# Preparing a chunk's two layouts with VectorE's 32x32 transposes instead of TensorE's, norms spread through DRAM

## The chip, the core and the metric

One core of a Trainium2 chip runs the whole program in one launch. The metric is the time of one execution on the device, in microseconds (us). Engines are named as the profile names them: PE (TensorE, matrix multiplication; PEld is its weight load), DVE (VectorE), ACT (ScalarE), POOL (GpSimd) and SP (SyncE, which here only issues transfers). Each engine works through its own instructions in order; semaphores make it wait for others.

## The reference

The input `x` has four images of 32 channels, 128x128 pixels, float32. Layer 0 is an attention among the positions that share a channel block: the image is regrouped so that 2x2 pixels become four channels, rows of a matrix `q` with 128 rows and 4096 columns per image, and the rest is

```python
xs = x.reshape(B, C, h, R, w, R).transpose(0, 1, 3, 5, 2, 4).reshape(B, C * R * R, h, w)
q = xs.reshape(B, C * R * R, hw)                   # 4 x 128 x 4096
energy = jnp.einsum('bci,bcj->bij', q, q)          # 4096 x 4096 per image
d = jnp.sqrt(jnp.diagonal(energy, axis1=1, axis2=2))
attn = jax.nn.softmax(energy / (d[:, :, None] * d[:, None, :]), axis=-1)
out = gamma * jnp.einsum('bcj,bij->bci', q, attn) + xs   # then back to the image
```

So every one of the 4096 columns of `q` is divided by its own norm before the product, and the values use `q` as it is. Layer 1 takes the image's pixels as 8 x 8192 tokens of 128 features: a linear attention over 8 heads after a layer norm, added to the tokens, then a layer norm and a mixture of 8 experts with the best two of a softmax router, added again. Only layer 0's preparation of `q` is touched by the change.

## The kernel before, in words

The kernel goes through the four images (batches, b = 0 to 3). A batch has 4096 columns in 8 chunks of 512 (`CH`); two chunks are prepared together, so a batch has four preparations, kc = 0 to 3. In this text a prepared pair is called "a chunk" where its preparation is meant. `prep` (lines 282 to 350) makes two layouts of it. `qT` holds columns on the partitions (128 columns by 128 channels, four such blocks per 512 columns) and is used as values; `qn` holds channels on the partitions with 512 normalised columns and is used on both sides of the energy product.

`prep` loads image rows into `xx` with four transfers of 128 KB (`load_tokens`, line 274), transposes them on PE into PSUM (`ptq`, line 313) and copies them with DVE into `qT` (line 302). DVE squares `qT` and sums the squares (lines 324, 325), POOL raises the sums to the power -1/2 (`pow_neg_half`, line 163), DVE scales `qT` with the result into `qs` (line 338), PE transposes `qs` (`ptn`, line 346), and ACT copies that into `qn` (line 344). Between these steps stand `yield`s.

`attend` (line 417) is the main work. For each chunk i and each jc up to i it multiplies `qn` with `qn` (`pe`, line 556), ACT takes the exponential into `pr` and sums its rows (line 559), and PE multiplies `pr` with `qT` (`po`, line 440). The energy is symmetric, so only half of it is made; for the other half DVE transposes `pr` in 32x32 blocks into `F` (line 369), SP writes `F` to DRAM as `blocks` (line 483) and reads it back regrouped as `G` (line 491), and `transposed_share` (line 371) multiplies `G` with `qT` into `pg` and adds that to the accumulator `o` of chunk jc (line 385), while ACT sums `G` (line 380). `po` becomes `o` by a copy of ACT (line 445).

The order of the instructions on PE, DVE, ACT and SP is that in which the program issues them (`manual_schedule`, line 1329). A step of `attend` is one exponential; `after(n, f)` issues `f` n steps later, and a share of `G` is issued when `clock`, which counts 128-column pieces of PE's work, has gone `LAG` = 57 pieces on. Other work runs along as generators: a list `timed` holds (generator, begin, end, count), with begin and end in per cent of a batch's `clock`, and `count` turns are spread over that window. `attend` yields twice in a step; the list `moved` of the generators to advance is made at the first of the two and used at both:

```python
for half, _ in enumerate(chain(attend(b, states[b]), ...)):
    if half % 2 == 0:
        moved = []
        ...                       # generators whose turn it is
    for steps in moved:
        next(steps, None)
```

So one turn takes a generator past two `yield`s. Layer 1 of the batch before runs in the same way (`layer1`, line 602): `close_rows` divides `o` by the softmax's sums and adds it to the tokens `T` (`divide`, line 703), then follow statistics on DVE, a power on POOL, a normalisation on ACT, PE products, the sorting of tokens by expert through DRAM (POOL's indirect transfers), the experts' products `pys`, and the sum with the tokens that ACT fetches back from DRAM (`fetch`, line 1097).

Buffers that the steps speak of: PSUM has two banks for `pe`, one for `po`, two for `pg` and three for everything else (`pt`, handed out by `hold`, line 191); `pr` has six buffers, `qT` five, `qn` ten, `xx` one; `T` holds a batch's rows, which `input_rows` (line 593) loads.

## Time and profile before

| what | us |
|---|---|
| three runs | 1710.81, 1708.52, 1704.93 |
| median | 1708.52 |
| the profiled execution | 1712.1 |
| its span, first to last instruction | 1710.3 |
| PE busy in it | 1651.3 |
| DVE busy | 934.7 |
| ACT busy | 925.2 |
| POOL busy | 512.0 |

The mean granted clock of TensorE is 0.994. A line of the groups reads: line of the kernel, engine, operation, names out<-in, size, xcount | busy us, mean ns of one | idle time of the engine just before them, and what ended it. A line in the order of time reads: start, length, engine, line, operation, [idle before it <- what ended that]. Ends of matmuls are modelled, and a matmul is shown until its last result, so two that follow each other overlap in the rows; the time that one takes of PE is read from start to start. "SPq" is a transfer's issue on SP's queue.

### The profile page before, as it was taken

The numbers are of one execution on the slowest core, as the hardware profiler recorded it, in microseconds if no ns is written. First come the engines' busy times: TensorE is split into PE (matmuls) and PEld (weight loads), VectorE is DVE, ScalarE is ACT, GpSimd is POOL, SyncE is SP. The second block draws the span as 40 slices with busy tenths as digits, with TensorE's granted clock in tenths as the row PEclk, the third lists the DMA queues.
The fourth block names the chain that finished last, engine by engine and source line by source line (L and its number), as shares of the span: only waits on it lengthen the run. The fifth ranks groups of instructions, "written<-read, shape, count | busy, mean of one in ns | idle before, by whom it ended". The sixth has DMA issues, their size and how long they took to land. (4 is left out here: it accounts for less than half of the span.)

```text
span 1710.3 us, 21189 instructions
## 1 busy us (share of the span) xinstructions
PE 1651.3 (97%) x5458; PEld 875.0 (51%) x5458; DVE 934.7 (55%) x2443; ACT 925.2 (54%) x2893; POOL 512.0 (30%) x553
## 2 busy tenths in 40 slices
PE   8999999999999999989999999999999999998897
PEld 5444444455554555445554455544555455554543
DVE  4433344467485345478478334547748533455686
ACT  3555445566565555546575555545556555554476
POOL 1000000011027425460015632544102642445166
PEclk9999999999999999999999999999999999999999
DMA  4665768876569888985568888997646987996001
GB/s 141 190 210 172 201 209 243 259 217 186 162 194 282 252 257 250 281 261 178 160 191 244 262 264 247 261 263 220 186 150 191 286 260 236 257 277 151 7 11 40
DMA packets 240681, 355.25 MB, mean 208 GB/s; under 512 B 27312, under 2 KB 155312, under 8 KB 226480
## 3 DMA queue, kind: packets, MB, share of 16 engines
q1 hardware_dynamic: 220048, 314.91, 62.4%
q0 software_dynamic: 12288, 25.19, 5.1%
q10 hardware_dynamic: 8224, 13.77, 2.8%
q8 instruction: 46, 0.75, 0.2%
q14 instruction: 75, 0.61, 0.1%
HBM read 183.64 MB, written 173.15 MB: 209 GB/s over the span
## 5 line engine op out<-in xcount | busy, mean ns | idle before, releaser
L559 ACT ACTIVATE pr<-pe 128x512 f32<-128x512 f32 (+1 forms) x576 | 322.4, 560 | 548.8 <-PE pe L556 432.0
L440 PE MATMUL po<-pr,qT 128*128 128x512 f32 (+3 forms) x1152 | 551.3, 560 | 3.9 <-ACT o L445 3.2
L556 PE MATMUL pe<-qn,qn 128*128 128x512 f32 x896 | 461.5, 597 | 3.8 <-ACT pr L559 2.7
L375 PE MATMUL pg<-G,qT 128*128 128x512 f32 x880 | 450.9, 594 | 4.1 <-DMA G<-blocks 4.1
L369 DVE STREAM_TRANSPOSE F<-pr 128x512 f32<-128x512 f32 x440 | 306.0, 702 | 163.3 <-ACT pr L559 140.9
L440 PEld LDWEIGHTS po<-pr,qT 128*128 128x128 f32 x1152 | 215.9, 191 | 250.4 <-issue 223.0
L380 ACT ACTIVATE junk<-G 128x512 bf16<-128x512 f32 x440 | 273.0, 621 | 2.6 <-DMA G<-blocks 2.6
L375 PEld LDWEIGHTS pg<-G,qT 128*128 128x128 f32 x880 | 167.2, 191 | 200.6 <-issue 185.1
L1122 POOL DMA_INDIRECT yb<-ys,place x192 | 185.9, 968 | 254.5 <-ACT pr L559 82.1
L995 POOL DMA_INDIRECT xs<-xn,place x192 | 186.3, 970 | 158.9 <-ACT pr L559 81.4
L556 PEld LDWEIGHTS pe<-qn,qn 128*128 128x128 f32 x896 | 153.9, 191 | 112.9 <-issue 100.0
L385 DVE TENSOR_TENSOR o<-o,pg 128x512 f32<-128x512 f32 x110 | 75.4, 685 | 192.3 <-PE pg L375 155.3
L164 POOL TENSOR_TENSOR rn<-ss,neg_half 128x8 f32<-128x8 f32 (+1 forms) x17 | 26.9, 1586 | 334.1 <-DVE ss L325 334.0
L559 ACT ACTIVATION_READ_ACCUMULATOR pr<-pe 128x1 f32 x576 | 112.2, 195 | 0.0
L1031 ACT ACTIVATE xn<-pys 128x256 f32<-128x256 f32 x120 | 45.3, 377 | 113.0 <-PE pys L1064 71.4
L164 POOL TENSOR_TENSOR rsf<-dm_f,neg_half 128x8 f32<-128x8 f32 (+1 forms) x15 | 26.2, 1748 | 233.6 <-DVE sv_f L636 233.6
L1057 PEld LDWEIGHTS pys<-ew_sb,xn 128*128 128x128 f32 x468 | 69.4, 191 | 49.0 <-issue 42.6
L556 PE MATMUL pe<-qn 128*128 128x512 f32 (+3 forms) x256 | 90.5, 436 | 4.0 <-ACT pr L559 3.3
L380 ACT ACTIVATION_READ_ACCUMULATOR junk<-G 128x1 f32 x440 | 84.5, 192 | 0.0
L164 POOL TENSOR_TENSOR rsa<-dm_a,neg_half 128x8 f32<-128x8 f32 x16 | 26.4, 1648 | 188.6 <-DVE sv_a L636 188.2
L1040 DVE COPY xn<-pys 128x256 f32<-128x256 f32 x60 | 25.4, 424 | 93.5 <-ACT xn L1031 72.3
L1040 DVE COPY result<-pys 128x256 f32<-128x256 f32 (+1 forms) x60 | 24.6, 410 | 90.4 <-ACT xn L1031 46.3
(212 smaller groups left out, 1653.5 us busy)
## 6 DMA issues: line engine op xcount, KB each, us to landing
blocks<-F SPq DMA_DIRECT2D x108, 1024.0 KB
G<-blocks SPq DMA_DIRECT2D x432, 256.0 KB
xn<-xs SPq DMA_DIRECT2D x114, 128.0 KB
below<-F SPq DMA_DIRECT2D x31, 384.0 KB
G<-below SPq DMA_DIRECT2D x124, 96.0 KB
out_dram<-acc SPq DMA_DIRECT2D x128, 64.0 KB
xx<-in_x_dram SPq DMA_DIRECT2D x62, 128.0 KB
ys<-xn SPq DMA_DIRECT2D x60, 128.0 KB
```

The source lines that it names most:

```text
L164: pinned(nc.gpsimd.tensor_tensor(dst, src, neg_half.to_broadcast(list(src.shape)), ALU.pow))
L369: f()
L375: nc.tensor.matmul(pg.rearrange("p (a f) -> p a f", a=4), st["qT"][i][:, ib, :], G[:, :, ib], start=(ib == 0), stop=(ib == NJ - 1),)
L380: nc.scalar.activation(junk, G[:, :, ib], AF.Copy, accum_out=st["sums"][:, NJ * i + ib, jc : jc + 1])
L385: nc.vector.tensor_tensor(o, o, pg.rearrange("p (a j c) -> p a j c", a=4, c=S), ALU.add)
L440: nc.tensor.matmul(row["po"][:, lo:hi], qT[blk // NJ][:, blk % NJ, :], w, start=start, stop=(row["left"] == 0))
L556: nc.tensor.matmul(pe[:, c0:], qn[jc][:, ts(j, P)], qn[i][:, c0:], start=True, stop=True)
L559: nc.scalar.activation(pr[:, c0:], pe[:, c0:], AF.Exp, accum_out=sums[:, t, i : i + 1]).ins
L995: inst = nc.gpsimd.indirect_dma_start(xs[h], offset(place[:, i, k : k + 1]), xn[:, k, :], None)
L1040: nc.vector.tensor_copy(result[:, :n], p[:, 2 * P : 2 * P + n * D].rearrange("p (j c) -> p j c", c=D))
L1057: nc.tensor.matmul(p[:, 2 * P + j * D : 2 * P + j * D + D], bufs[4 + g % 2][:, j, :], weights[:, bass.ds(begins[2 * (g % 2) + j], D)], sta ...
L1122: inst = nc.gpsimd.indirect_dma_start(yb[k // 4][:, i, k % 4, :], None, ys, offset(place[:, i, k : k + 1]))
```

## The change

Both layouts are now made without PE, except for the first chunk of the first batch.

- `load_quarters` loads image rows so that 32 partitions hold the 32 channels and four such groups hold four rows each (`xa`, four transfers of 128 KB, two pieces of 2 KB per partition in each). `turn_quarters` transposes them with DVE in 32x32 blocks straight into `qT`: four instructions of 256 elements per partition for a chunk. The columns come in another order than before.
- Squares, sums and the power stay. The power's result lies in a [128, 32] tile whose other columns hold ones; DVE transposes it, ACT's queue writes it to DRAM (`norms`, 16 KB) and reads it back twice, each time spread over 64 partitions (`wide`). DVE multiplies image rows with `wide` into `qn`: four instructions of 64 partitions by 512 (`scale`).
- The image rows for that are loaded as before, as `xx` from the second batch on, after the quarters have been turned, into the same buffer. In the first batch they go straight into `T`, and `input_rows` no longer loads `T` there.
- `ahead` is the number of `yield`s between a transfer and its use: five, and two for the second chunk.
- The first chunk has `prep_first`: DVE transposes the quarters, the scaled `qs` goes through PE and ACT as before. The spare transposes that keep PE running are 40, before 22.
- The accumulator `o` has its columns in the order of `pg`: ACT permutes when it copies `po` into `o`, the add of `pg` is plain, the adds of `back` and `divide` permute.
- The windows of the preparations and their counts change: 26 turns instead of 12 or 13.

```diff
+    def load_quarters(b, kc, queues=(nc.sync, nc.sync)):
+        xa = xin.tile([P, 2, 2, 2, HW2, 2], F32, tag="xx", name=f"xa_{b}_{kc}")
+        halves = x[b].rearrange("c (s g) w -> c s (g w)", s=2)
+        for a in (0, 2, 1, 3):
+            first_row = 16 * kc + 4 * a
+            queues[a // 2].dma_start(
+                xa[ts(a, S)].rearrange("p s k r w e -> p s (k r w e)"),
+                halves[:, :, first_row * W : (first_row + 4) * W],
+            )
+        return xa
+
+    def turn_quarters(s, xa, qT):
+        for k in range(2):
+            nc.vector.transpose(
+                qT[:, s, 2 * k : 2 * k + 2, :].rearrange("p h (e r c) -> p r (h e) c", e=2, r=2),
+                xa[:, s, k].rearrange("p r (h t) e -> p (r h) e t", h=2),
+            )
...
+    def squares(b, kc, s, qT, ss):
+        sq = work.tile([P, NJ, P], F32, tag="qs", name=f"sq_{b}_{kc}_{s}", bufs=2)
+        nc.vector.tensor_tensor(sq, qT[:, s], qT[:, s], ALU.mult)
+        nc.vector.tensor_reduce(ss[:, ts(s, NJ)], sq, AX.X, ALU.add)
...
     def prep(b, kc, st):
...
-                    nc.tensor.transpose(
-                        pt[:, ts(2 * jj + r2, P)], xx[:, k : k + 2, :, r2].rearrange("p k w -> p (k w)"), ident
-                    )
...
+        ahead = 2 if b == 0 and kc == 1 else 5
+        xa = load_quarters(b, kc)
+        if b == 0:
+            load_tokens(st["T"][:, ts(kc, 8), :], b, 8 * kc, 8)
+            xx = rows_of_image(b, kc, st)
+        for _ in range(ahead):
+            yield
+        qT = chunks_of(b, kc, st)
+        for s in range(2):
+            turn_quarters(s, xa, qT)
+            yield
+        if b > 0:
+            xx = xin.tile([P, 8, HW2, 2], F32, tag="xx", name=f"xx_{b}_{kc}")
+            load_tokens(xx.rearrange("p k w r -> p k (w r)"), b, 8 * kc, 8)
...
+        def scale(s, spread, view):
+            qn = channels(b, kc, s, st)
+            own = slice(s * 64, s * 64 + 64)
+            for r2 in range(2):
+                nc.vector.tensor_tensor(
+                    qn[ts(r2, 64)].rearrange("p (j a t) -> p a j t", a=4, t=S),
+                    xx[own].rearrange("p (a k) (h t) r -> p r a (k h) t", a=4, h=2)[:, r2],
+                    view(spread[own]),
+                    ALU.mult,
+                )
+        norm = norms[kc % 2]
+        for s in range(2):
+            squares(b, kc, s, qT, ss)
+            if s == 1:
+                pow_neg_half(norm[:, : 2 * NJ], ss)
+            yield
+        for _ in range(ahead - 2):
+            yield
+        turned = stat.tile([P, S], F32, tag="turned", name=f"turned_{b}_{kc}")
+        nc.vector.transpose(turned, norm)
         yield
+        kept = dram.tile([P, S], F32, tag="norms", name=f"norms_{b}_{kc}")
+        nc.scalar.dma_start(kept, turned)
+        for _ in range(ahead):
+            yield
+        wide = work.tile([P, CH], F32, tag="qs", name=f"wide_{b}_{kc}", bufs=2)
+        for s in range(2):
+            nc.scalar.dma_start(
+                wide[ts(s, 64)].rearrange("p (a f) -> p a f", a=4),
+                kept.rearrange("(a q) t -> a (q t)", q=S)[:, ts(s, P)].partition_broadcast(64),
+            )
+        for _ in range(ahead):
+            yield
+        for s in range(2):
+            scale(s, wide, lambda ap: ap.rearrange("p (a j t) -> p a j t", a=4, t=S))
+            yield
...
-                o = st["o"][jc].rearrange("p (j a c) -> p a j c", a=4, c=S)
-                nc.vector.tensor_tensor(o, o, pg.rearrange("p (a j c) -> p a j c", a=4, c=S), ALU.add)
+                nc.vector.tensor_tensor(st["o"][jc], st["o"][jc], pg, ALU.add)
...
-                    nc.scalar.activation(o, row["po"], AF.Copy)
+                    nc.scalar.activation(in_order(o), in_turn(row["po"]), AF.Copy)
...
-            for kc, begin, end in ((1, 0, 5), (2, 6, 20), (3, 25, 45)):
-                timed.append((prep(0, kc, states[0]), begin, end, 12))
+            for kc, begin, end in ((2, 6, 22), (3, 25, 48)):
+                timed.append((prep(0, kc, states[0]), begin, end, 26))
...
-            timed.append((prep(b + 1, 0, nxt), 65, 82, 13))
-            timed.append((prep(b + 1, 1, nxt), 87, 99, 13))
+            timed.append((prep(b + 1, 0, nxt), 52, 78, 26))
+            timed.append((prep(b + 1, 1, nxt), 80, 99, 26))
...
-            timed.append((prep(b + 1, 2, nxt), 2, 20, 13))
-            timed.append((prep(b + 1, 3, nxt), 30, 50, 13))
+            timed.append((prep(b + 1, 2, nxt), 1, 22, 26))
+            timed.append((prep(b + 1, 3, nxt), 28, 52, 26))
```

## The prediction

> **What bounds the kernel now.** I read the page's busy times and slices first, then the groups of instructions, then the order in time around the work that the change removes, and last the waits of that work.
>
> ```profile
> PE 1651.3 (97%) x5458; PEld 875.0 (51%) x5458; DVE 934.7 (55%) x2443; ACT 925.2 (54%) x2893; POOL 512.0 (30%) x553
> PE   8999999999999999989999999999999999998897
> DVE  4433344467485345478478334547748533455686
> DMA  4665768876569888985568888997646987996001
> ```
>
> PE is busy in 97% of the span and in nearly every slice; DVE and ACT are at 55% and 54%. So an instruction taken off PE is worth its own time, if nothing else makes PE wait. DMA is at nine tenths in several slices.
>
> The order in time around two of the removed groups, and the rows of the DVE work on both sides of the change:
>
> ```profile
> 1322.71 1.02 PE L375 MATMUL pg<-G,qT 128*128 128x512 f32 x2
> 1323.57 0.63 PE L313 MATMUL ptq<-ident,xx 128*128 128x128 f32 x4
> 1324.04 1.02 PE L556 MATMUL pe<-qn,qn 128*128 128x512 f32 x2
> ...
> 1354.62 1.02 PE L375 MATMUL pg<-G,qT 128*128 128x512 f32 x2
> 1355.48 0.60 PE L346 MATMUL ptn<-ident,qs 128*128 128x128 f32 x4
> 1355.91 1.02 PE L556 MATMUL pe<-qn,qn 128*128 128x512 f32 x2
> ```
> ```profile
> L369 DVE STREAM_TRANSPOSE F<-pr 128x512 f32<-128x512 f32 x440 | 306.0, 702 | 163.3 <-ACT pr L559 140.9 <-issue 14.8 <-DMA G<-blocks 5.5
> L513 DVE STREAM_TRANSPOSE F<-pr 128x128 f32<-128x128 f32 x186 | 44.0, 282 | 26.6 <-ACT pr L559 25.9 <-ACT junk L380 0.5 <-issue 0.2
> L709 DVE TENSOR_TENSOR df<-o,pbd 64x512 f32<-64x512 f32 x64 | 43.9, 686 | 8.6 <-PE pe L556 3.9 <-PE pbd L722 3.5
> L302 DVE COPY qT<-ptq 128x512 f32<-128x512 f32 x32 | 21.7, 679 | 33.1 <-PE ptq L313 26.7 <-PE pe L556 6.4
> L338 DVE TENSOR_TENSOR qs<-qT,rn 128x512 f32<-128x512 f32 x32 | 20.6, 682 | 1.5 <-POOL rn L164 1.5
> ```
>
> PE has no gap here. From start to start, four ptq transposes take 0.47 us of it and four ptn transposes 0.43 (the shown 0.63 and 0.60 overlap what follows). The places where PE did wait at this work, in the order of time:
>
> ```profile
> 726.98 0.72 PE L313 MATMUL ptq<-ident,xx 128*128 128x128 f32 x4 [1.38 <-DMA xx<-in_x_dram]
> 749.73 0.66 PE L346 MATMUL ptn<-ident,qs 128*128 128x128 f32 x4 [2.77 <-issue]
> 1135.20 1.10 PE L313 MATMUL ptq<-ident,xx 128*128 128x128 f32 x4 [3.77 <-issue]
> 1160.71 0.66 PE L346 MATMUL ptn<-ident,qs 128*128 128x128 f32 x4 [3.07 <-DVE o L385]
> ```
> ```profile
> 376.42 1.91 SPq L279 DMA_DIRECT2D xx<-in_x_dram  x4
> 1121.65 10.25 SPq L279 DMA_DIRECT2D xx<-in_x_dram  x4
> ```
> ```profile
> 490.00:500.00 10.00, 9.45 (x26) 4.47 (x25) 9.43 (x42) 4.83 (x15) 2.11 (x3) 1.00 0.76 211
> ```
>
> Two waits are for input rows that came late, two for DVE. The four loads of one chunk took 1.9 us to issue in a quiet stretch and 10.25 in a dense one, where SP waits for earlier transfers between them. The last row (columns: window, length, busy PE, PEld, DVE, ACT, POOL, clock, DMA share, GB/s) is the stretch where DVE is nearly full.
>
> **Removed from PE.** 16 chunks lose two ptq groups each and 15 lose two ptn groups (the first chunk keeps its own). Outside the start that is 30 x 0.47 = 14.1 us and 30 x 0.43 = 12.9 us, together 27.0, all on the path of an engine that is full. The four waits above, 1.38 + 2.77 + 3.77 + 3.07 = 11.0, lose the instructions that waited; I count them as gone here and price what is late next below. ACT loses 30 evictions of 0.59 (17.7 us), off the path. The permuted accumulator costs nothing: the permuted add at L385 takes 685 ns and the contiguous one at L524 684, so the change swaps equals; ACT's permuted copy into o is bounded by L445's 590 and L380's 621 ns, 32 x 0.03 = 1 us on an engine half idle.
>
> **The start.** PE's first pe starts at 13.62 us, after rows (5.70), transposes, copy, squares, sums, power, scaling. Without the first transposes and copies (5.70 to 8.38), but with four DVE transposes, three of which stand ahead of the first square, the first scaling ends about 1.4 us sooner: -1.4. The 40 spare transposes (0.2 us each by 22 in 4.4 us) fill 8 us in which PE has nothing; if they begin only at 5 us they end at 13 and the gain is gone. The second chunk uses two steps of distance, about 3 us for each of its two transfers, against 2.8 us from the last issue at 724.15 to use at 726.98: I take +1 (bounds 0 and 4, one late transfer of 3.6 us as at 1131.58 to 1135.20).
>
> **Added to DVE.** A 128x256 transpose lies between 282 ns (128x128) and 702 (128x512): 0.49, four a chunk, 1.97. Four scalings of 64x512 at 0.686 are 2.74, the norms' transpose at most 0.28, say 0.2. Against two copies and two scalings removed (2.72), a chunk costs DVE 2.2 us more: 33 us over 15 chunks. 55% becomes 57%; by itself hidden. It lies on a path in one place: for the chunk prepared in the window 28 to 52% of a batch, two of the transposes stand in DVE's order ahead of the statistics whose POOL result ACT awaits (ACT idle 4.15 us at 496.47, PE 0.55 at 498.74 already). 2 x 0.49 = 1 us each in batches 1 to 3: +3 (bounds 0 and 9, if the squares' 2.7 us also count).
>
> **The new waits.** The loop that advances a chunk's generator moves it twice per turn (the list of what moves is kept over the second half step), so five steps are 2.5 turns of 1/26 of the window. A batch is 405 us (ptq at 390.69, then 796.16), so transfer to use is 7.4 us in the window 80-99, 8.2 in 1-22, 9.3 in 28-52, 10.1 in 52-78; before it was 3.5 turns of 1/13: 13.1 us in 87-99. There the rows came 1.38 and 3.77 late, so they took 14.5 and 16.9 us from step to landing. With 7.4 us DVE, not PE, now stands 7.1 to 9.5 us at two chunks, before the transposes of pr, the adds of pg and the copies of pys that are queued behind. PE goes on while six pr tiles, two pg and three pt banks last; the pr tiles give some four steps of 2.58 us, 10 us, the pt banks less. Bounds 0 and 9.5; I take 3 each: +6. In these two chunks the first transpose also waits for a matmul two steps ahead (5.2 us), beside this wait, not on top. In window 1-22, the first issue stood 5.3 us behind its step before (3.5 turns of 1/13 of 2-20 are 19.6; 376.42 to 390.69 is 14.3), then 1.9 issue and 2.8 landing: 10.0 against 8.2, DVE waits 1.8; PE through the closing of layer rows 0 to 2, I take 1, three times: +3.
>
> ACT issues 45 DMAs (norms out, two rows back). An issue itself lies beside an ACTIVATE (313.41 within 313.19 to 313.79), cost nothing; a wait in it holds the exponentials queued behind, and PE after two pe banks. It waits for DVE's transpose, for the norms' landing, and for earlier SP transfers with the same semaphore. The 24 fetches of t2 by ACT show no PE wait; the largest unexplained ACT gap (4.53 us at 769.54) cost PE 3.05. Bounds 0 and 3.05 x 15 = 46; nearest are the 24 fetches, so a tenth: +4.
>
> SP issues 60 quarter loads more, 32 half-size loads of batch 0 less. Bytes: +8.4 MB quarters, +4.2 norms out and spread, -2.1 second read of batch 0: 10.5 of 355, 3%. SP's blocks and G transfers are queued behind these loads; PE waits 4.1 us for late G now (2.31 at 188.05). I take +2 (bounds -1 and 12 x 2.31 = 28).
>
> **Sum.** -27.0 - 1.4 - 11.0 = -39.4; +1 +3 +6 +3 +4 +2 = +19. The profiled execution took 1712.1 us (span 1710.3), so 1691.7; it lies 3.6 above the median of the runs, so 1688.
>
> Two rules of the Trainium skill speak against the change. "VectorE: DVE Perf Modes", section Rules for kernel authors, sends a 128x128 transpose to TensorE if PSUM will do; the row here is 0.47 us of a full PE plus 0.68 of DVE against about 0.98 of a DVE with room. If the rule held here, the 14.1 us would not be earned and the sum would be 1702. "DMA: Bandwidth & Descriptors", section Specifications, puts line rate at 512 B and more; the norms leave in rows of 128 B. No row of this trace shows that alone; were it to double the 2.8 us, ACT would wait half a microsecond for three chunks, and the sum would be 1690.
>
> **Rivals.** (1) All of the gain stays: DVE's waits end within PE's buffers, ACT's never bind. For it: in quiet stretches rows land in time, and DVE has 45% idle. Against: dense stretches. 1712.1 - 39.4 - 3.6 = 1669. (2) No difference: ACT's wait for norms or for SP's transfers costs PE 3.05 us at 12 chunks, 36.6: 1706. For it: order on ACT is strict, and two steps of 2.58 us is the shortest distance from norms out to norms back. Against: the fetches. (3) Slower: each of the 12 chunks of batches 1 to 3 holds DVE for its rows longer than PE's buffers last. It decides from 39.4 / 12 = 3.3 us of PE a chunk; at 4.53 it gives 1712.1 - 39.4 + 54.4 - 3.6 = 1723. For it: distances are halved, and DVE is full at 490. Against: outside 80-99 SP issued the rows in 2 to 3 us.
>
> **How the numbers follow.** Forecast 0.52 (1676 to 1702), rival 1 0.13, rival 2 0.10, rival 3 0.25. A measurement tells about 0.3%, 5 us. Faster takes the forecast and rival 1, same nearly all of rival 2, slower rival 3. The range goes from 1667, rival 1's end, into rival 3 up to 1718. Median time: 1688.
>
> **What would show it.** Right: no ptq groups, PE busy near 1620, most of the four waits gone, DVE near 965, ACT near 907, DVE idle before the new transposes mostly in 80-99. Wrong: PE waiting for pr or pg after DVE idle on xa at many chunks (3); ACT idle on norms or a remote wait (2); G late more than twice.

## The result, and the profile after

The change makes the kernel slower. The kernel after takes 1738.22 us (median of four runs, 1736.35 to 1739.5), the kernel before 1709.66 in the runs that it was compared with: a ratio of 1.0146 (95% interval 1.0119 to 1.0173). The prediction said 1688, with a range of 1667 to 1718. The profiled execution after took 1739.5 us, its span is 1737.7, which is 27.4 above the span before.

The page of the kernel after, busy times and slices:

```profile
span 1737.7 us, 20825 instructions
PE 1646.1 (95%) x5228; PEld 855.5 (49%) x5228; DVE 958.4 (55%) x2520; ACT 909.4 (52%) x2863; POOL 510.9 (29%) x555
...
PE   8999999899999999899999999979999999999898
...
DVE  4443343467485444568477353457748533454686
...
DMA  4767867786559999896667998888655988895001
```

The reader expects PE's busy time to fall by the work removed; it fell only from 1651.3 to 1646.1, in a longer span. Busy time hides two things here: instructions that ran at half clock count twice, and idle time is not in it. So I take the span apart with the windows view, one row per microsecond: idle is a window's length less PE's busy time in it; clock loss is (1 - granted clock) x busy; what is left is PE's work at full clock. (The view rounds each row to 0.01 us; summed, idle comes out up to 0.9 us under the span less the page's busy time.)

| kernel | span | PE idle | clock loss | PE work at full clock |
|---|---|---|---|---|
| before | 1710.3 | 58.7 | 8.0 | 1643.6 |
| after | 1737.7 | 90.9 | 23.8 | 1623.0 |
| difference | +27.4 | +32.2 | +15.8 | -20.6 |

The work did go: 20.6 us less, and 24.2 less if the 18 more spare transposes at the start (0.2 each) are set aside. Idle time and the clock took back more than twice that. PE's idle time by what ended it, first lines of that view, kernel after:

```profile
PE pg L436 <- DMA G<-blocks: 26.7, 6, 8.3
PE pe L617 <- ACT pr L620: 17.3, 10, 2.9
PE po L500 <- ACT o L505: 6.1, 15, 2.2
PE pys L1124 <- DMA xn<-xs: 5.4, 6, 2.2
...
PE pcnt L1009 <- DVE runs L1000: 2.7, 3, 0.9
```

The columns are us in total, times, longest. In the same view of the kernel before:

```profile
PE pe L556 <- ACT pr L559: 6.0, 7, 3.1
PE pg L375 <- DMA G<-blocks: 4.1, 2, 2.3
PE po L440 <- ACT o L445: 3.2, 12, 0.5
PE pys L1064 <- DMA xn<-xs: 2.9, 5, 1.2
```

Late `G` rose by 22.6 us, late `pr` by 11.3. Six waits make the first number, and three of them four fifths of it, each in the window 80 to 99 of a batch, where the prediction had put DVE's waits. Order of time, kernel after:

```profile
342.52 2.05 PE L436 MATMUL pg<-G,qT 128*128 128x512 f32 x2 [6.11 <-DMA G<-blocks]
...
739.52 2.04 PE L436 MATMUL pg<-G,qT 128*128 128x512 f32 x2 [6.95 <-DMA G<-blocks]
...
1155.56 2.05 PE L436 MATMUL pg<-G,qT 128*128 128x512 f32 x2 [8.30 <-DMA G<-blocks]
```

These two matmuls last 1.02 us elsewhere; here 2.05. The windows around the first of the three (kernel after; window, length, busy PE, PEld, DVE, ACT, POOL, granted clock, DMA share, GB/s) show why:

```profile
338.00:340.00 2.00, 0.00 (x0) 0.00 (x0) 1.92 (x7) 0.00 (x0) 0.00 (x0) 0.98 0.98 216
340.00:342.00 2.00, 0.00 (x0) 0.00 (x0) 0.46 (x1) 0.00 (x0) 0.00 (x0) 0.50 1.07 349
342.00:344.00 2.00, 1.48 (x2) 0.84 (x3) 0.00 (x0) 0.72 (x2) 0.00 (x0) 0.50 0.58 246
344.00:346.00 2.00, 2.00 (x3) 0.68 (x2) 0.00 (x0) 0.00 (x0) 0.00 (x0) 0.50 0.07 14
346.00:348.00 2.00, 2.00 (x5) 0.86 (x4) 0.00 (x0) 1.30 (x4) 0.00 (x0) 0.81 1.03 249
348.00:350.00 2.00, 2.00 (x9) 1.15 (x8) 1.22 (x2) 0.37 (x1) 0.00 (x0) 1.00 0.99 223
```

After PE has stood, the granted clock is 0.50, and it stays there after the work is back. Such a stretch lasts 3.41 us, or twice that, 6.83. The kernel before has four of them in its span before the end, the kernel after 14; each costs 1.6 to 2.9 us of busy time, and the ten more make the 15.8. In the kernel after they follow stalls of 1.94 to 8.30 us (the last, at 1664.30, one of 0.69), but not every such stall has one: PE stood 2.90 us up to 1399.49 and 2.23 up to 23.40 with the clock full behind it. The Trainium skill's page "TensorE: Matmul & The Clock Gate", section "Part 1: The HAM clock gate", describes a clock with two states, half and full, that is decided in free-running windows of 3413 ns and falls after an idle one; the 0.50 and the 3.41 us here agree with it. The condition for the fall does not: here stalls of 1.94 to 3.02 us, shorter than a window, were enough in ten places.

### The profile page after: what moved, and what is told of

Read it like the earlier page. It is cut to its first block, busy times and chain, and to the rows that moved or that the text cites. A ratio compares the mean times of both kernels' runs of the same rounds, so it can differ in the third digit from the quotient of the medians.

```text
span 1737.7 us, 20825 instructions
## 1 busy us (share of the span) xinstructions
PE 1646.1 (95%) x5228; PEld 855.5 (49%) x5228; DVE 958.4 (55%) x2520; ACT 909.4 (52%) x2863; POOL 510.9 (29%) x555
## 4 chain that ended last, share of the span: by engine, by line
PE 64%; DMA 11%; DVE 9%; issue 6%; ACT 3%; SPq 3%; another core or an unknown queue 1%; POOL 1%; ACTq 0%; DVEq 0%; POOLq 0%
PE pe L617 19%; PE po L500 18%; PE pg L436 15%; DMA G<-blocks 3%; PE py L1266 2%; PE pys L1117 2%; DMA blocks<-F 2%; PE pgram L736 2%; PE pg L456 2%; DMA xn<-xs 1%; PE pat L862 1%; DVE F L424 1%; SPq L551 1%; PE pys L1124 1%
## 5 line engine op out<-in xcount | busy, mean ns | idle before, releaser
L617 PE MATMUL pe<-qn,qn 128*128 128x512 f32 x896 | 467.5, 604 | 15.2 <-ACT pr L620 14.7
L436 PE MATMUL pg<-G,qT 128*128 128x512 f32 x880 | 454.3, 598 | 28.4 <-DMA G<-blocks 26.7
L617 PEld LDWEIGHTS pe<-qn,qn 128*128 128x128 f32 x896 | 157.7, 193 | 142.4 <-issue 108.6
L164 POOL TENSOR_TENSOR norm<-ss,neg_half 128x8 f32<-128x8 f32 x15 | 24.8, 1651 | 375.1 <-DVE ss L296 375.1
L1091 ACT ACTIVATE xn<-pys 128x256 f32<-128x256 f32 x120 | 45.3, 377 | 123.4 <-PE pys L1124 72.4
L164 POOL TENSOR_TENSOR rsa<-dm_a,neg_half 128x8 f32<-128x8 f32 x16 | 26.4, 1649 | 188.9 <-DVE sv_a L696 188.8
L1151 DVE SCALAR_TENSOR_TENSOR acc<-yb,weight,acc 128x128 f32<-128x128 f32 x192 | 65.4, 342 | 17.9 <-DMA yb<-ys,place 13.7
L1100 DVE COPY xn<-pys 128x256 f32<-128x256 f32 x60 | 25.3, 421 | 90.7 <-ACT xn L1091 68.2
```

The source lines that it names most:

```text
L164: pinned(nc.gpsimd.tensor_tensor(dst, src, neg_half.to_broadcast(list(src.shape)), ALU.pow))
L436: nc.tensor.matmul(pg.rearrange("p (a f) -> p a f", a=4), st["qT"][i][:, ib, :], G[:, :, ib], start=(ib == 0), stop=(ib == NJ - 1),)
L617: nc.tensor.matmul(pe[:, c0:], qn[jc][:, ts(j, P)], qn[i][:, c0:], start=True, stop=True)
L1151: nc.vector.scalar_tensor_tensor(a[:, k % 4, :], yb[k // 4][:, i, k % 4, :], weight[:, i, k, :], a[:, k % 4, :], ALU.mult, ALU.add)
```

## The experiments

Two theories stood at first. One: what holds `G` back is SP, which stands in the new second load `xx` because its transfers wait for ACT's new norms transfers. The other, rival 3 of the prediction: the steps between transfer and use are too few, so DVE stands for rows or norms and everything behind it comes late. Later runs test what the first ones left. Every ratio is against the kernel before, run beside it on the same chip. There were five such groups; ratios are compared inside a group only, for a reason that the last group shows. Idle, clock loss and work are the columns of the table above, for the experiment's own trace.

| group | kernel | ratio (95%) | span | idle | clock | work |
|---|---|---|---|---|---|---|
| 1 | spread | 1.0172 (1.0145, 1.0199) | 1736.0 | 93.0 | 25.3 | 1617.7 |
| 1 | no_xx | 1.0093 (1.0068, 1.0119) | 1710.2 | 72.4 | 17.8 | 1620.0 |
| 1 | no_norms | 1.0040 (1.0017, 1.0063) | 1704.2 | 69.6 | 14.6 | 1620.0 |
| 1 | half_ptn_spread | 1.0068 (1.0040, 1.0096) | 1719.3 | 71.8 | 16.1 | 1631.4 |
| 2 | norms_pool | 1.0046 (1.0025, 1.0067) | 1700.0 | 66.9 | 15.2 | 1617.9 |
| 2 | norms_sp | 1.0039 (1.0021, 1.0058) | 1706.1 | 70.9 | 17.4 | 1617.8 |
| 2 | later | 1.0107 (1.0077, 1.0137) | 1708.4 | 76.3 | 13.0 | 1619.1 |
| 2 | last84 | 1.0095 (1.0059, 1.0132) | 1708.1 | 75.6 | 14.5 | 1618.0 |
| 3 | all3 | 1.0002 (0.9987, 1.0016) | 1695.5 | 65.8 | 13.2 | 1616.5 |
| 3 | all3_pe | 1.0078 (1.0056, 1.0100) | 1710.1 | 57.2 | 12.5 | 1640.4 |
| 3 | half_moved | 0.9889 (0.9869, 0.9909) | 1681.8 | 44.8 | 9.6 | 1627.4 |
| 3 | bare | 0.9901 (0.9880, 0.9923) | 1681.2 | 53.0 | 15.8 | 1612.4 |
| 4 | act_hold | 1.0226 (1.0189, 1.0263) | 1747.5 | 100.0 | 26.4 | 1621.1 |
| 4 | xx_after | 1.0113 (1.0077, 1.0149) | 1723.3 | 83.5 | 18.6 | 1621.2 |
| 4 | half_moved2 | 0.9939 (0.9916, 0.9962) | 1701.3 | 62.0 | 8.1 | 1631.2 |
| 5 | after_same_chip | 1.0110 (1.0078, 1.0141) | 1729.8 | 88.9 | 16.4 | 1624.5 |
| 5 | pool_same_chip | 1.0208 (1.0181, 1.0236) | 1742.4 | 95.3 | 25.9 | 1621.2 |
| 5 | hold_same_chip | 1.0151 (1.0126, 1.0176) | 1735.3 | 91.3 | 21.8 | 1622.2 |

A span is one execution and a ratio is of medians, so the two can differ by some us (8.5 in no_xx: profiled 1711.95, median 1720.47).

### Longer distances (spread)

```diff
-                timed.append((prep(0, kc, states[0]), begin, end, 26))
+                timed.append((prep(0, kc, states[0]), begin, end, 13))
...
-            timed.append((prep(b + 1, 1, nxt), 80, 99, 26))
+            timed.append((prep(b + 1, 1, nxt), 80, 99, 13))
...
```

Half as many turns in each of the five windows, so every distance is twice as long.

> The changed kernel took 1738. One edit: the preparations in the main loop get 13 turns in their windows instead of 26, so that two steps a turn use up the whole window and every distance between a transfer and its use doubles (window 80 to 99 per cent: 14.8 us instead of 7.4). Theory 1, distances too short: xa, xx, norms and G come in time; the three long waits for G (6.11, 6.95 and 8.30 us, 21.4 together) go to about 1 us each, and with them some 3 us of half clock: 1738 - 18 - 3 = 1717, and less (about 1705) if the three waits of 2.39 us for pr in the window 28 to 52 go too. Theory 2, DVE's added instructions hold it up wherever they stand: the waits for pr stay or move, 1730 or more. Theory 3, the added bytes fill the DMA engines: G stays late, 1730 or more.

Measured: 1.0172. DVE's waits for rows (`xa`) fell from 19.5 us in 6 to 7.6 in 4, those for norms (`wide`) from 7.5 to 3.9, and PE's idle time did not fall (93.0). Late transfers moved elsewhere. SP's order and PE's order in that stretch of spread:

```profile
517.67 0.37 SPq L543 DMA_DIRECT2D blocks<-F  x1
518.09 9.64 SPq L279 DMA_DIRECT2D T<-in_x_dram  x4
528.05 1.39 SPq L551 DMA_DIRECT2D G<-blocks  x2
```
```profile
525.84 1.02 PE L617 MATMUL pe<-qn,qn 128*128 128x512 f32 x2
532.25 1.22 PE L500 MATMUL po<-pr,qT 128*128 128x512 f32 x1 [5.39 <-DMA G<-blocks]
```

SP now stood 9.64 us in the loads of `T` with the fetch of `G` behind them, and PE 5.39, in each of batches 1 to 3 (5.95, put down to `o`, and 5.36 in the others). So with most of DVE's wait for its rows gone the kernel is as slow, and rival 3 in the prediction's form is not borne out; the new waits are of the edit's own making, so this run alone does not exclude it.

### Without the second load, without the norms (no_xx, no_norms)

```diff
-            xx = xin.tile([P, 8, HW2, 2], F32, tag="xx", name=f"xx_{b}_{kc}")
-            load_tokens(xx.rearrange("p k w r -> p k (w r)"), b, 8 * kc, 8)
+            xx = xa.rearrange("p s k r w e -> p (s k r) w e")
```

> The changed kernel without the second load of a chunk from the second batch on: DVE scales the quarters xa in place of the rows xx (other values, the same instructions), so 48 transfers of 128 KB on SP's queue are left out (6.3 MB of 366). Theory 1a, SP's queue is held by the xx loads (7.40 us at 320.82, 8.22 at 1130.25) and blocks and G stand behind them: the three long waits for G lose at least two thirds, 14 us, and some clock: about 1720. Theory 1b, DVE's waits for xa hold F, and so G: those waits stay, 1735. Theory 3, bytes: 1.7 per cent fewer, little change, 1733 or more.

```diff
-        nc.scalar.dma_start(kept, turned)
...
-            nc.scalar.dma_start(
-                wide[ts(s, 64)].rearrange("p (a f) -> p a f", a=4),
...
-            scale(s, wide, lambda ap: ap.rearrange("p (a j t) -> p a j t", a=4, t=S))
+            scale(s, flat, lambda ap: ap.to_broadcast([64, 4, NJ, S]))
```

> The changed kernel without the way of the norms through DRAM: qn is scaled with a constant, so ACT's queue issues 45 transfers less; DVE, POOL and SP keep their instructions and the steps keep their number. Theory 4, ACT's waits for the norms and the transfers of other queues that wait behind norms and wide (SP waited 7.8, 6.5, 3.9 us for them) cause the late G: the three waits lose half or more, and the waits for pr at 978.97 and 1399.49 go: about 1718. Theory 1a or 2: 1732 to 1738.

Both kernels leave work out: no_xx scales the quarters in place of the rows, no_norms scales with a constant. Measured: 1.0093 and 1.0040. Taking the norms away does more for the time than taking the second load away, and neither brings the time of the kernel before. What the norms do can be seen at a place. SP's order in the kernel after, at the second load of the chunk prepared in window 80 to 99:

```profile
318.98 1.73 SPq L551 DMA_DIRECT2D G<-blocks  x4
320.82 7.40 SPq L279 DMA_DIRECT2D xx<-in_x_dram  x4
328.32 0.53 SPq L543 DMA_DIRECT2D blocks<-F  x1
335.10 1.74 SPq L551 DMA_DIRECT2D G<-blocks  x4
```

and the same load in no_norms:

```profile
310.76 1.84 SPq L279 DMA_DIRECT2D xx<-in_x_dram  x4
```

Four transfers take SP 7.40, 7.75 and 8.22 us in batches 0 to 2 of the kernel after and 1.84 to 1.91 without the norms; behind them stand `blocks` and `G`. Of SP's waits in the kernel after, 64.6 us in 18 waits are for ACT's new transfers, the norms. The longest of these groups:

```profile
SPq L551 <- DMA norms<-turned: 23.5, 5, 6.5
...
SPq L566 <- DMA norms<-turned: 17.5, 3, 7.8
```

SP uses none of these norms. In the program both queues draw on one set of completion counts, so a transfer of SP waits until the earlier transfer of ACT that had the same count has landed; 43 of ACT's 45 new transfers have an SP transfer waiting for them in this way.

SP waited for ACT's transfers before the change too. In the kernel before, 70.7 us in 19 of its waits are for ACT's older transfers (31.4 for `xs<-in_x_dram`, 27.1 for `acc<-t`, the rest for weights); one of them, 6.1 us for `acc<-t`, lies in a load of `xx` that took 9.75 us at 714.72. In the kernel after these older waits are 28.2 us in 10. So SP's waits for ACT rose by 22 us in all, and what is new is also their place: in batches 0 to 2 they hold the second load of window 80 to 99, with `blocks` and `G` behind it.

The sum of PE's three waits before a `pg` matmul in window 80 to 99 (in some traces one is put down to DVE) is 21.4 us in the kernel after (19.6 in its second trace, after_same_chip) and 11.6 to 14.6 in all six traces with this window in which no norms go through ACT's queue: no_norms 11.6, norms_pool 12.9, norms_sp 12.1, act_hold 13.3, pool_same_chip 14.6, hold_same_chip 11.6. The run later (below), which keeps ACT's queue and this window, has 17.7. In one and the same group the difference is 5.2 us (17.7 against 12.9 and 12.1) or 6.5 (19.6 against 14.6 and 11.6); the means of the first two and of the six are 20.5 and 12.7. So 5 to 8 us of the late `G` is this coupling. Without the second load it does not show at these waits: in no_xx, where the norms still go through ACT's queue, they are 9.8 us. The remainder, in no_norms (PE, then DVE):

```profile
722.40 2.04 PE L428 MATMUL pg<-G,qT 128*128 128x512 f32 x2 [4.42 <-DMA G<-blocks]
...
1128.07 1.72 PE L428 MATMUL pg<-G,qT 128*128 128x512 f32 x2 [4.33 <-DMA G<-blocks]
```
```profile
697.02 1.45 DVE L316 STREAM_TRANSPOSE qT<-xa 128x256 f32<-128x256 f32 x4 [7.40 <-PE po L492]
```

DVE's first transpose of the chunk waits until PE has done with the `qT` buffer that it writes, and the `F` transposes from which `G` is made are queued behind. That this makes `G` late is read from the order of the rows; no run isolates it. The prediction named this wait ("also waits for a matmul two steps ahead") and put it beside the wait for rows, at no cost.

### A scaled half by PE, with long distances (half_ptn_spread)

```diff
-                timed.append((prep(0, kc, states[0]), begin, end, 26))
+                timed.append((prep(0, kc, states[0]), begin, end, 13))
...
-            xx = xin.tile([P, 8, HW2, 2], F32, tag="xx", name=f"xx_{b}_{kc}")
...
-            nc.scalar.dma_start(
...
+            qs = work.tile([P, NJ, P], F32, tag="qs", name=f"qs_{b}_{kc}_{s}", bufs=2)
+            nc.vector.tensor_tensor(qs, qT[:, s], rn[:, ts(s, NJ)].to_broadcast([P, NJ, P]), ALU.mult)
...
+            pt, done = hold(f"ptn_{b}_{kc}_{s}", lambda p, qn=qn: nc.scalar.activation(qn, p, AF.Copy))
+            for j in range(NJ):
+                nc.tensor.transpose(pt[:, ts(j, P)], qs[:, j, :], ident)
```

`qT` still comes from DVE's transposes of quarters; `qn` is made as in the kernel before, with no second load and no norms through DRAM.

> Half of the change: qT by DVE's transposes of the quarters, but qn as before by four PE transposes and a copy of ACT (no second load from the second batch on, no norms through DRAM), 13 turns a window. PE saves 30 groups of ptq, 14.1 us, and the waits before the ptq groups (1.38 and 3.77). If a PE transpose group is worth its time: 1709.7 - 14 - 3 = 1693. If DVE's transposes ahead of the statistics cost what they save, or waits come back elsewhere: 1705 to 1710.

Measured: 1.0068, against 1.0172 of spread in the same group (medians 1717.62 and 1736.57): half of the change with the same long distances is 19 us better than all of it, although it has 13.7 us more PE work.

### The norms by another queue (norms_pool, norms_sp)

```diff
-        nc.scalar.dma_start(kept, turned)
+        nc.gpsimd.dma_start(kept, turned)
...
-            nc.scalar.dma_start(
+            nc.gpsimd.dma_start(
```

norms_sp has `nc.sync` in both places.

> The changed kernel with the 45 transfers of the norms issued by POOL instead of ACT; nothing else. Theory 4a: a transfer's issue waits for the one before it that counts on the same completion semaphore; SP's and ACT's transfers share eight of them and so SP, ahead in the program's order, waits for norms that ACT has not yet issued; POOL's have their own eight. Then xx issues in about 1.9 us (as without the norms) and the time falls to that of the run without norms, 1712, plus POOL's own waits: 1712 to 1720. Theory 4b, the norms' bytes and their landing: qn comes as late as before, 1730 or more. Theory 4c, POOL's waits for the norms hold the powers behind them: slower than 1738.

> The changed kernel with the 45 transfers of the norms issued by SP instead of ACT. If ACT's waits (2.7 us for turned at 323.67, 3.06 at 721.51), which hold the exponentials, are what costs: faster, about 1725. If SP's waits for the norms are what costs (theory 4a): they stay, since SP now waits for DVE's turned and the landing itself, and blocks and G stand behind it: 1735 or more.

Measured: 1.0046 and 1.0039, beside 1.0107 and 1.0095 of the two kernels of this group that keep ACT's queue and have one other edit each. `xx` is issued in 1.84 to 1.92 us in the windows 80 to 99 of both. For norms_sp this is a miss of its expectation, by which SP's waits would stay (1735 or more): SP does wait there for the norms and the transposed tile, 33.7 us in 17 waits, but after `xx` and not in it, and late `G` is 12.1 us as said above. The kernel after itself was not in this group, but both kernels near it are slower than the two without ACT's queue. Group 5 says otherwise of the total time, below.

### Two windows moved (later, last84)

```diff
-            timed.append((prep(b + 1, 3, nxt), 28, 52, 26))
+            timed.append((prep(b + 1, 3, nxt), 36, 60, 26))
```

> The changed kernel with the window 28 to 52 moved to 36 to 60, same length and turns; nothing else. Theory: in the window 28 to 52 the transposes and squares (0.73 + 2.7 us) stand in DVE's order ahead of the sorting's probabilities, for which ACT and then PE wait (2.39 us at 512.94, 923.36 and 1342.06, and 0.9 before it for the runs, and half clock behind it, 1.7): 3 x 5.0 = 15 us go, 1723. If DVE is late there for another reason, or the work meets the loads of input rows at 36 to 47 instead: 1733 to 1740.

The place that this edit is about, in the kernel after (DVE, ACT, PE):

```profile
502.04 0.73 DVE L316 STREAM_TRANSPOSE qT<-xa 128x256 f32<-128x256 f32 x2
...
504.92 0.65 DVE L295 TENSOR_TENSOR sq<-qT 128x512 f32<-128x512 f32 x1
505.60 0.69 DVE L296 TENSOR_REDUCE ss<-sq 128x4 f32<-128x512 f32 x1
506.20 0.68 DVE L295 TENSOR_TENSOR sq<-qT 128x512 f32<-128x512 f32 x1
506.92 0.69 DVE L296 TENSOR_REDUCE ss<-sq 128x4 f32<-128x512 f32 x1
...
511.68 0.29 DVE L897 TENSOR_TENSOR prob<-lg,weight 128x128 f32<-128x128 f32 x1
```
```profile
512.00 0.31 ACT L898 ACTIVATE prob<-prob 128x128 f32<-128x128 f32 x1 [3.53 <-DVE prob L897]
```
```profile
512.94 1.13 PE L617 MATMUL pe<-qn,qn 128*128 128x512 f32 x2 [2.39 <-ACT pr L620]
```

and in the kernel before, where ACT waited 0.38 us there:

```profile
502.40 0.31 ACT L838 ACTIVATE prob<-prob 128x128 f32<-128x128 f32 x1 [0.38 <-DVE prob L837]
```

Two transposes, two squares and two sums, 3.4 us of DVE, now stand between the layer norm and the router's `prob`, which an exponential of ACT awaits; PE waits 2.39 us at 512.94, 923.36 and 1342.06, and the clock is halved after each. Measured for later: these three waits are gone, and the largest `pe` wait in those stretches is the 0.55 that the kernel before has too:

```profile
495.08 1.12 PE L617 MATMUL pe<-qn,qn 128*128 128x512 f32 x2 [0.55 <-ACT pr L620]
```

But PE now waits for sorted rows instead (`xn<-xs`, 3.13 us at 576.23, 1.99 at 677.37, 1.93 at 984.62), and the ratio is 1.0107, where its expectation had a gain of 15 us. The cause of the 2.39 is shown; that moving the work away earns it is not.

```diff
-            timed.append((prep(b + 1, 1, nxt), 80, 99, 26))
+            timed.append((prep(b + 1, 1, nxt), 84, 99, 26))
```

> The changed kernel with the window 80 to 99 moved to 84 to 99, same turns; nothing else. DVE's first turn of that chunk waited 7.72 and 10.75 us in batches 1 and 2 for a buffer of qT that PE's po still read; 4 per cent later, 16 us, it is free. If this wait is what makes G late (the chain pr, F, blocks, G): the waits of 6.95 and 8.30 lose half or more, 1725. If SP's waits for the norms make it late: they stay, 1735 or more.

Measured: 1.0095. DVE's wait before the first transpose fell from 10.75 to 4.79 us in batch 2 and is now for `xa`, but two `G` waits stand where one stood (PE, last84):

```profile
722.94 2.04 PE L436 MATMUL pg<-G,qT 128*128 128x512 f32 x2 [4.44 <-DMA G<-blocks]
738.65 1.10 PE L436 MATMUL pg<-G,qT 128*128 128x512 f32 x2 [3.51 <-DMA G<-blocks]
```

One wait for a buffer was exchanged for a wait for rows at a distance that is now shorter.

### All three, and PE's work put back (all3, all3_pe)

all3 has the norms on POOL's queue and both moved windows. all3_pe is all3 with two groups of four transposes on PE for each half of a chunk, which nobody uses:

```diff
+    def spare_group():
+        pt, done = hold("spare", lambda p: None)
+        for j in range(NJ):
+            nc.tensor.transpose(pt[:, ts(j, P)], ident, ident)
+        done()
...
+            spare_group()
```

> The changed kernel with the three edits together: norms issued by POOL, window 28 to 52 at 36 to 60, window 80 to 99 at 84 to 99. If the three causes are separate, their gains add: from the ratios to before (1.0146 changed; 1.0046, 1.0107 and 1.0095 with one edit each) 1.0146 - 0.0100 - 0.0039 - 0.0051 = 0.9956, which is faster than before by 7 us. If each edit alone is cut short by the next wait in the same place, the sum of waits counts: the run with norms by POOL still has 4.80 and 5.16 for G, 2.91 for DVE in the first batch, 3 x 3.3 for pr and runs, and some 5 us of half clock, 28 together: ratio 0.988. If late bytes are the limit, G stays late and the ratio is 1.000 or more.

> The kernel with the three edits, and where a chunk is turned and where it is scaled four transposes of the identity into a free PSUM bank, two groups each: the 60 groups that the change took from PE are put back as bare PE work, which nothing waits for. If a group is worth its time from start to start (0.47 and 0.43, prediction), this is 27 us slower than the kernel with the three edits. If PE has idle time in which they hide: less than 15.

Measured: 1.0002 and 1.0078. The 1.0002 misses both gains that were thought possible and is the third case, late `G`: the trace of all3 has waits for it of 6.81, 4.07 and 3.84 us. That bytes are the reason is not shown; no run varies them alone. The 60 groups are 23.9 us of PE's work (1640.4 - 1616.5), 0.40 us each, and the median rose by only 12.5 (1713.64 - 1701.11): idle time fell by 8.6, clock loss by 0.7. So a microsecond of these transposes is worth about half a microsecond of time, in this kernel. That is measured; why is only argued: a share of `G` is issued `LAG` = 57 pieces after its exponential, and pieces count only the main work, so less other work between leaves the chain `pr`, `F`, `blocks`, `G` less time.

### Half of the change (half_moved, half_moved2), and all of it without transfers (bare)

half_moved is half_ptn_spread with 26 turns again and the two moved windows (36 to 60, 84 to 99). bare is all3 with flat norms and no second load, so it adds no transfers but the quarter loads:

```diff
-            xx = xin.tile([P, 8, HW2, 2], F32, tag="xx", name=f"xx_{b}_{kc}")
-            load_tokens(xx.rearrange("p k w r -> p k (w r)"), b, 8 * kc, 8)
+            xx = xa.rearrange("p s k r w e -> p (s k r) w e")
...
-            scale(s, wide, lambda ap: ap.rearrange("p (a j t) -> p a j t", a=4, t=S))
+            scale(s, flat, lambda ap: ap.to_broadcast([64, 4, NJ, S]))
```

> Half of the change (qT by DVE, qn by PE and ACT as before; no second load, no norms through DRAM), with 26 turns in the windows and the two windows at 36 to 60 and 84 to 99. Theory 4a: nothing couples the queues, so no late G from it; PE saves 30 groups, 14 us, and the waits of 1.38 and 3.77: ratio 0.990, about half of what the full change could bring. If the loads alone make G late: 1.000 or more.

> The kernel with the two windows moved, and neither the norms' transfers nor the second loads (qn scaled by a constant from the quarters): the change's work on PE and DVE without its new transfers, except the quarters. This is what rival 1 of the prediction called all of the gain: 1712.1 - 39.4 of 1712.1, ratio 0.977. If DVE's added 2.2 us a chunk, or the quarters' loads, cost something wherever they stand: 0.985 or more.

Measured: half_moved 0.9889 (1682.87 us against 1702.77), the best kernel of this study, about 20 us faster than the kernel before; bare, which leaves out the norms, 0.9901. No run moves the windows in the kernel before, so how much of the 20 us is theirs is open. bare has 15 us less PE work than half_moved and is no faster: it idles 8.2 us more and loses 6.2 more to the clock. Against all3, leaving out the norms' round trip and the second load is worth 17.0 us (1701.11 - 1684.07) in the same group: that is what the transfers cost, even with the windows moved and the norms on another queue. The page and the waits of half_moved:

```profile
PE 1636.1 (97%) x5348; PEld 864.4 (51%) x5348; DVE 936.3 (56%) x2475; ACT 927.0 (55%) x2893; POOL 512.2 (30%) x555
```
```profile
PE pg L419 <- DMA G<-blocks: 11.2, 3, 4.9
PE pgram L719 <- ACT xn L687: 6.0, 3, 2.6
```

Late `pr` is not among its first four waits, though DVE stands as long for its quarters (20.9 us in 6) as in the kernel after (19.5 in 6).

```diff
-            timed.append((prep(b + 1, 1, nxt), 84, 99, 26))
+            timed.append((prep(b + 1, 1, nxt), 82, 99, 13))
```

> The half change with the windows moved, and for the last chunk 82 to 99 with 13 turns instead of 84 to 99 with 26: its distances double. DVE's wait of 4.38 us for the quarters at 702.13 goes, and if it makes G late, the waits for G of 3.69 and 4.95 us and 4 us of half clock: ratio 0.983. If G is late because the DMA engines are full there: 0.988 to 0.990, as before this edit.

Measured, in another group: half_moved2 0.9939. This is neither of the expected ratios: PE's waits for late `G` are shorter (2.55 us the longest, 4.95 in half_moved), the ratio is not better. Whether the longer distance or the group makes the difference to 0.9889 is open; both are faster than the kernel before.

### ACT's wait, and the second load later (act_hold, xx_after)

act_hold issues the norms by POOL but leaves ACT the wait for the turned norms:

```diff
-        nc.scalar.dma_start(kept, turned)
+        nc.gpsimd.dma_start(kept, turned)
+        held_up = stat.tile([P, 1], F32, tag="held_up", name=f"held_{b}_{kc}")
+        nc.scalar.activation(held_up, turned[:, 0:1], AF.Copy)
```

> The changed kernel with the norms issued by POOL, and where ACT issued them an ACT copy of one column of turned: ACT waits for DVE as in the changed kernel, but no transfer of ACT's queue stands between SP's. If ACT's wait held the exponentials and that was the cost: back to 1.012 to 1.015 of before. If SP's wait for the norms' transfers was: it stays at that of the norms by POOL, 1.0046, give or take 0.002.

xx_after issues `xx` after ACT's norms transfer and not before the squares:

```diff
-        if b > 0:
-            xx = xin.tile([P, 8, HW2, 2], F32, tag="xx", name=f"xx_{b}_{kc}")
...
         nc.scalar.dma_start(kept, turned)
+        if b > 0:
+            xx = xin.tile([P, 8, HW2, 2], F32, tag="xx", name=f"xx_{b}_{kc}")
...
```

> The changed kernel (norms on ACT's queue) with the second load of a chunk issued after the norms' transfer in the program's order instead of right after the quarters are turned, some five steps later. If SP's wait for the norms is the cost: xx issues in 2 to 4 us instead of 7.4 to 8.2, blocks and G come earlier, ratio near that of the run without xx, 1.009, or less. If ACT's wait is: 1.0146. If the norms are still not issued when SP comes to xx, the wait only moves: 1.012 or more.

Measured: 1.0226 and 1.0113. The first is far above the 1.0046 that norms_pool had in group 2. xx_after issues `xx` in 2.1 to 2.4 us, but SP then waits for the norms at `G` (27.1 us in 5 waits at L551): the wait moved to the next transfer in SP's order. Its ratio tells nothing, as no kernel of its group is the kernel after.

### The same three on one chip (after_same_chip, pool_same_chip, hold_same_chip)

The kernel after, norms_pool and act_hold, unchanged, beside each other.

> The changed kernel again, on the same chip as the next two. If the edits judged on another chip were judged rightly, its ratio to before is 1.012 to 1.017 here too. If the chip made the difference: under 1.008 on a chip without unexplained waits.

> The norms issued by POOL, on the same chip as the changed kernel. If the norms on ACT's queue are what costs: 0.8 to 1.1 per cent under the changed kernel, on any chip. If the earlier ratio (1.0046) was the chip's: within 0.3 per cent of it.

> The norms issued by POOL and ACT's wait for turned put back, on the same chip. Theory SP (SP waits for counts that norms hold): as the norms by POOL, within 0.3 per cent. Theory ACT (exponentials behind ACT's wait): as the changed kernel or slower. If it is the unexplained waits that made it slow: slow only if this chip's traces have them.

Measured: 1.0110, 1.0208 and 1.0151. Putting ACT's wait back (hold) shows no cost against pool; as the difference has the other sign, the totals cannot weigh a few us here. Nothing points to the 36.6 us of rival 2. And the same program, norms issued by POOL, has 1.0046 in group 2 and 1.0208 here. Between its two traces lie 42.4 us: 28.4 of PE's idle time, 10.7 of clock, 3.3 of work. One place in pool_same_chip, ACT and SP:

```profile
617.81 0.19 ACT L441 ACTIVATION_READ_ACCUMULATOR junk<-G 128x1 f32 x1
625.23 0.38 ACT L1091 ACTIVATE xn<-pys 128x256 f32<-128x256 f32 x1 [7.22 <-remote]
```
```profile
616.64 2.85 SPq L551 DMA_DIRECT2D G<-blocks  x4
625.22 0.38 SPq L1081 DMA_DIRECT2D xn<-xs  x1
```

ACT and SP start again within 0.01 us of each other after 7.22 and 5.7 us in which the profile names no releaser of this core ("remote" is its name for another core or an unknown queue). The same instruction in norms_pool's trace:

```profile
622.59 0.38 ACT L1091 ACTIVATE xn<-pys 128x256 f32<-128x256 f32 x1 [0.66 <-PE pys L1124]
```

All eight traces of groups 2 and 3 have no such wait on any engine; all ten of groups 1, 4 and 5 have them, 4 to 13 on ACT, and so have the first traces of before (6 on ACT, 20.7 us) and after (7, 27.9 us). The number of the chip does not tell them apart: the record has chip 0 for group 2 and for group 5. What PE stood right behind them is 6.2 us in the first trace of before and 8.3 in that of after (16.1 in pool_same_chip), so directly they make 2 of the first pair's 27.4; what they make by later `G` is not shown. Nor is the loss without them: the kernel after was not run in group 2 or 3, and the nearest to it there, later and last84, have 1.0107 and 1.0095. What causes these waits was not found; no run here varied it. Because of them I do not say what moving the norms off ACT's queue is worth in total: its 5 to 8 us at the `G` waits are there in both kinds of trace, its ratio is not.

## Why the prediction was wrong, by its own steps

The differences of the two first traces, in the prediction's terms (us; "other waits" is the rest, and includes the start):

| step | predicted | measured |
|---|---|---|
| work removed from PE | -27.0 | -24.2 |
| four waits gone | -11.0 | -11.0 |
| late `G` (SP's loads) | +2 | +22.6 |
| window 28 to 52 | +3 | +8.3 |
| half clock after stalls | none | +15.8 |
| start -1.4, second chunk 1, window 80-99 6, window 1-22 3, ACT 4; measured: other waits and spares | +12.6 | +15.9 |
| sum | -20.4 | +27.4 |

**Removed from PE.** The groups are gone and the instruction count says so. Their price was close: 0.40 us a group by all3_pe against the 0.47 and 0.43 taken. What failed is the sentence that an instruction taken off PE is worth its own time: as many groups, put back as bare work in all3, cost 12.5 us, not 23.9. Argued, as above: part of PE's other work was covering the way of `G`.

**The four waits.** Gone, as predicted, and "what is late next" was priced at the wrong engine: the rows came late to DVE as expected (19.5 us in 6 waits), but what PE stood for was `G`. (5.66 of them are the start.)

**SP and late `G`: the step that failed most.** The prediction counted SP's loads and their bytes, took +2 with an upper bound of 28, and named the sign (late more than twice: six times). The bound held, the choice in it did not. It also wrote that ACT's transfers wait "for earlier SP transfers with the same semaphore" and did not ask the reverse, an SP transfer that waits for ACT's. The trace of before shows it, in a stretch that the prediction read as dense: at 714.72 a load of `xx` took 9.75 us, 6.1 of them a wait for ACT's `acc<-t`, and the late `ptq` of 726.98 used that load. (Nor is it so that outside window 80 to 99 the rows were issued in 2 to 3 us: the load at 246.59 took 8.46, 5.1 of them a wait for ACT's `xs`.) The runs put 5 to 8 of the 22.6 us on this coupling; for the remainder the traces show DVE's first transpose standing 7.40 us (no_norms) and 7.72 (after) for `po` to leave the `qT` buffer, with `F` behind it, but no run isolates this, and how the remainder divides stays open. The prediction counted that wait at nothing because another stood beside it.

**The clock.** The sum had no such term, although the trace of before shows it: four stretches at 0.50, and the 1.10 us of the late `ptq` group at 1135.20, quoted in the prediction, lies in one of them. A stall costs its own length and then, where the clock falls, 1.6 to 2.9 us more.

**Window 28 to 52.** The mechanism was right and the bound named its cause ("if the squares' 2.7 us also count"): they count. PE waits 2.39 us for `pr` and 0.9 for the tokens' ranks (`pcnt`) in each of three batches, 9.9; in the kernel before it waited 1.6 in these stretches (0.55, 0.54, 0.54). So +8.3, just below the upper bound of 9.

**Window 80 to 99 and 1 to 22.** Before the first transpose of window 80 to 99 DVE stood 5.12, 7.72 and 10.75 us, about the 7.1 to 9.5 predicted, but at three chunks and not two; only the first is put down to `xa`, the second to `po`, the third to an output transfer (the instruction itself waits for `po` and `xa`). In window 1 to 22 it stood 0.44 and 2.92 against 1.8. The lengths were nearly right; what PE then lacked was not `pr`, which has six buffers, but the `G` made from it. Twice the distance took away three fifths of the waits for `xa` with no gain.

**DVE's price, ACT's transfers.** Rows of the kernel after:

```profile
L374 DVE TENSOR_TENSOR qn<-xx,wide 64x512 f32<-64x512 f32 x48 | 32.6, 680 | 0.5
L316 DVE STREAM_TRANSPOSE qT<-xa 128x256 f32<-128x256 f32 x64 | 23.0, 412 | 38.0 <-DMA xa<-in_x_dram 19.5 <-DMA out_dram<-acc 10.8 <-PE po L500 7.7
```

The transpose took 412 ns where 490 was estimated, the scaling 680 where 686 was; DVE is at 958.4 (965 said) and ACT at 909.4 (907). The +4 for ACT's waits was about 2: ACT waits three times for the transposed norms (2.65, 2.72 and 2.41 us), and behind the first PE stands 2.23 us at 23.40 for `o`, in the chunk for which the prediction took +1; behind the other two it stands 0.25 us and nothing. With the wait put back PE stands 2.17 us at that place (hold_same_chip), without it 0.18 (pool_same_chip).

**The start.** The first `pe` came 1.74 us sooner (11.88 against 13.62; 1.4 was predicted). But PE stood 2.30 us between the last spare transpose and `ptn`, and the clock fell at 12.25, which cost 1.7.

**The rules weighed.** The Trainium skill's rule that sends a 128x128 transpose to TensorE ("VectorE: DVE Perf Modes", Rules for kernel authors) is not borne out by half_moved, which makes `qT` on DVE and is 1.1% faster than the kernel before; its windows also differ, so the transposes are not alone in that, and half_ptn_spread, with other windows, is 0.7% slower. The price of short rows in the norms' transfer was not isolated by any run.

**The rivals.** Rival 1's full gain did not come even without the new transfers: bare has 0.9901, where 0.977 was expected of it. Rival 3 had the side and half of the size (1723, 14.5 above the 1708.52 of before; measured +28.6), but not the cause: its sign was PE waiting for `pr` or `pg` after DVE's idle on `xa` at many chunks, and three long waits on `G` with the clock behind them carry the loss. Sign (2) came true with rival 2 untrue: ACT has waits named "remote" in both kernels.

## What to carry to other kernels

Before a transfer is put on a second queue, look at which completion counts the program gives it: an issuing engine that shares them waits for transfers it does not use, and everything behind it in its order comes late; the waits of the issuing queue in the old trace show whether it does so already. On a full PE, ask of removed work what it was covering, and price each new PE stall at its length plus the half-clock time that can follow. A change of several parts should be tried in halves: here the half that moves `qT` to DVE with no new round trip through DRAM, its windows moved as well, was 1.1% faster, and the whole was 1.5% slower. Moving the windows alone was not tried.

## What was not expected of the hardware

The clock at half for 3.41 us (or twice that) 14 times in one execution, after stalls as short as 1.94 us (one after 0.69), while others of 2.23 to 2.90 us passed without it. And one program with ratios of 1.0046 and 1.0208 against the same kernel before, with waits of up to 7.2 us in the slower trace that the profile puts on no engine or queue of this core; that stays open.
